# VectorE's table and angle steps dealt into other places of the gate loop, one pair of gathers exchanged, and the first loads cut smaller, in a four-layer AdaLN/FFN kernel

## The chip, the cores and the metric

The kernel runs on one core of one Trainium2 chip, in one launch. The metric is the device time of that core in microseconds (us). A core has TensorE (PE; its weight loads are listed apart as PEld), VectorE (DVE), ScalarE (ACT), GpSimd (POOL) and SyncE (SP). Transfers (DMAs) are issued from the queues of SP, ACT and POOL. Each engine works through its own instructions in order and waits on semaphores for the others.

## The reference

Eight sequences of 128 tokens of width 512 pass four layers, each of two steps, each layer added to its input:

```python
x = x + _L0_ffn_ref(_L0_cond_ref(x, ..., itok_B_2_6, 0), ...)
x = x + _L1_ffn_ref(_L1_cond_ref(x, ..., itok_B_3_7), ...)
x = x + _L2_ffn_ref(_L2_cond_ref(x, ..., itok_Bx16_0_63, itok_B_207_1644), ...)
x = x + _L3_ffn_ref(_L3_cond_ref(x, itok_B_0_7, ...), ...)
```

The change touches the inside of two of them. The first step of layer 0 is a gated feed-forward net of width 1376 with a low-rank adapter per sequence:

```python
def lora_add(base, inp, A, B):
    Ab = A[layer_idx][lora_indices]
    Bb = B[layer_idx][lora_indices]
    t = jnp.einsum('bri,bni->bnr', Ab, inp)
    return base + jnp.einsum('bor,bnr->bno', Bb, t) * SCALE
gate = lora_add(jnp.einsum('bnh,fh->bnf', x, W_gate), x, A_gate, B_gate)
up = lora_add(jnp.einsum('bnh,fh->bnf', x, W_up), x, A_up, B_up)
act = jax.nn.silu(gate) * up
down = lora_add(jnp.einsum('bnf,hf->bnh', act, W_down), act, A_down, B_down)
```

The first step of layer 2 is attention over a paged cache: queries and keys are normed and rotated by position, cached keys and values are found by a block table, and cached positions beyond a sequence's length are masked:

```python
pos = cache_seqlens[:, None] + jnp.arange(seqlen)[None, :]
q = _rope(q, pos)
k = _rope(k, pos)
kc = k_cache[block_table].reshape(bsz, L, HK, D)
vc = v_cache[block_table].reshape(bsz, L, HK, D)
```

The other layers are adapters and routed mixtures; the change reaches them only through two small tables (`mask1`, `bias3`).

## The kernel before

All of x stays on the chip, turned: four chunks `c` of 128 features by 1024 tokens. A quarter is 256 tokens.

*Start.* SP loads the first 512 tokens chunk by chunk (L85), the adapter numbers `ids0_i` behind the first chunk (L88), then the remaining 512 tokens in one load of 1 MB (L89) and the weights of gate block 1 (L80). ACT loads the weights of block 0 in two pieces each for gate and up: chunk 0, then chunks 1 to 3. Loads from SP and ACT draw on the same eight semaphores, in turn, so that a load's issue waits until the load eight places earlier has landed. TensorE runs five matmuls on zeros (`idle`) and then block 0 (`gates`): for quarters 0 and 1, then 2 and 3, chunk by chunk, gate and up weights against each quarter. From `ids0_i` VectorE works out a row per partition, and GpSimd gathers the adapters' rows (Ag, Au, Bg, Bu, Ad, Bd).

*Tables.* `ints` loads the other id lists and turns them to floats (L134). From them VectorE builds `mask1`, `bias3` and, for values and for keys, the row numbers of the cache (`selp`, `page`, eight `kvrow` slices each, L180 to L191). They stand in the program ahead of the gate loop.

*Gate loop.* Blocks f = 1 to 10 of 128 hidden features (`gates_by_seven`) use Strassen's seven products. A block has for each of two groups `g` the banks `one`, `two` and `six`. TensorE runs the first products of both groups; VectorE makes three sums for each group from them (L456, L457, L459: six sums); TensorE then adds further products into the same banks, for which it must wait until VectorE has read them; the low-rank parts follow; then VectorE makes ten operations (L474 to L479) with ACT's Silu. Those ten run while TensorE is in the next block. The eight banks of PSUM go round, six to a block. GpSimd forms the weight sums of the next block (`weight_sums`, L429), and once, after block 5, sums of the down weights (L520). The order within each engine is written out by hand (`kept`). The rotation angles (`rotary`: `pos`, `ang`, then the reduction for sine and cosine, then small scalings of the norm weights) are 23 VectorE steps, dealt three at a time to the end of the blocks from f = 2 on.

*Attention.* 32 steps, each one group of heads for two sequences. A step n is prepared one step ahead: its projection (`project`, seven products again, `q_one`, `q_six`, `q_five`) and the product with the output weights of the step before (`leave`, `wo_one`, `wo_two`, `wo_six`) stand between the scores of two sequences. Cached keys are gathered by GpSimd (`gather(n, "k")`, eight indirect DMAs into `kn`), transposed by VectorE (`turn_cached`, L1111) and turned by a trip through memory; cached values are gathered into `vals`. GpSimd also makes the crossed rotation terms (`vq`, `vk`, L1070). At the start, `run` issues `gather(1, "v")` ahead of step 0, and `gather(2, "k")` in the middle of step 0; step 2's keys are transposed inside step 2's projection, which stands in step 1 (the entry "c22" there).

Of the kernel before, what the change touches and what calls it, by code (L numbers as in the profile page):

```python
# [10 lines left out]
F32 = mybir.dt.float32  # L11
I32 = mybir.dt.int32
AF = mybir.ActivationFunctionType
ALU = mybir.AluOpType
AX = mybir.AxisListType
PSUM = bass.MemoryType.PSUM

P = 128
NB = 8
NT = NB * P  # L20
D = 512
DC = D // P
# [6 lines left out]
NQ = 8  # L29
# [18 lines left out]
def forward(ctx: ExitStack, tc: tile.TileContext, a: dict, out: bass.AP):  # L48
    nc = tc.nc
    pe, act, dve, pool, sp = nc.tensor, nc.scalar, nc.vector, nc.gpsimd, nc.sync  # L50
# [23 lines left out]
    def gate_weights(f, by=sp, parts=(slice(0, DC),)):  # L74
        fw = min(P, FF - f * P)
        fs = slice(f * P, f * P + fw)
        ws = [st.tile([P, DC, P], F32, tag="w" + n, name=f"w{n}_{f}") for n in "gu"]
        for cs in parts:
            for n, w in zip("gu", ws):
                by.dma_start(w[:, cs, :fw], a[f"W{n}T"].rearrange("(c p) o -> p c o", p=P)[:, cs, fs])  # L80
        return ws

    ids0_i = const.tile([P, NB], I32, tag="lora_ids_i", name="lora_ids_i")
    for c in range(DC):
        sp.dma_start(x[:, c, 0:512], a["xT"][c * P : (c + 1) * P, 0:512])  # L85
        if c == 0:
            first = gate_weights(0, act, (slice(0, 1), slice(1, DC)))
            sp.dma_start(ids0_i, a["lora_ids"].partition_broadcast(P))  # L88
    sp.dma_start(x[:, :, 512:NT], a["xT"].rearrange("(c p) t -> p c t", p=P)[:, :, 512:NT])  # L89
    second = gate_weights(1)  # L90
# [39 lines left out]
    def ints(name, n, where=const):  # L130
        ti = where.tile([P, n], I32, tag=name + "_i", name=name + "_i")
        sp.dma_start(ti, a[name].partition_broadcast(P))
        tf = where.tile([P, n], F32, tag=name, name=name)
        dve.tensor_copy(tf, ti)  # L134
        return tf

    def rows(name, n, where=const):
        t = where.tile([P, n], F32, tag=name, name=name)
# [31 lines left out]


    mask1 = const.tile([P, NB], F32, tag="mask1", name="mask1")
    dve.tensor_scalar(mask1, ids1, p_div16, None, ALU.is_equal)

    kvrow = {}
    for what, order in (("v", "p (b c j) -> p b c j"), ("k", "p (b j c) -> p b c j")):
        selp = w0.tile([P, NB, 4, 4], F32, tag="selp", name="selp_" + what)
        dve.tensor_tensor(  # L180
            selp,
            table.rearrange(order, b=NB, c=4),
            block32.unsqueeze(1).unsqueeze(1).to_broadcast([P, NB, 4, 4]),
            ALU.mult,
        )
        page = const.tile([P, NB * 4], F32, tag="page", name="page_" + what)
        dve.tensor_reduce(page.rearrange("p (b c) -> p b c", c=4), selp, AX.X, ALU.add)
        dve.tensor_scalar(page, page, 32.0, p_mod32, ALU.mult, ALU.add)
        kvrow[what] = const.tile([P, NQ, NB * 4], I32, tag="kvrow_" + what, name="kvrow_" + what)
        for qd in range(NQ):  # L190
            dve.tensor_scalar(kvrow[what][:, qd, :], page, float(NQ), float(qd), ALU.mult, ALU.add)  # L191


    bias3 = const.tile([P, NB, 8], F32, tag="bias3", name="bias3")
    dve.tensor_tensor(
        bias3,
        eight.unsqueeze(1).to_broadcast([P, NB, 8]),
        lang.unsqueeze(2).to_broadcast([P, NB, 8]),
        ALU.is_equal,
    )  # L200
    dve.tensor_scalar(bias3, bias3, 5.0, None, ALU.mult)


    def load_small(dst_pool, name, shape, src, tag=None, bufs=None):
# [113 lines left out]
    with c0:  # L318
# [36 lines left out]
        def quarter(j):  # L355
            return slice(j * NT // 4, (j + 1) * NT // 4)
# [4 lines left out]
        def mmq(o, lhsT, rhs, start, stop):  # L361
            pe.matmul(o, lhsT, rhs, start=start, stop=stop, skip_group_check=True)  # L362
# [31 lines left out]
        def gates(f, ws, between):  # L394

            fw = min(P, FF - f * P)
            banks = [bank(f"gu_{f}_{j}") for j in range(4)]
            for js in ((0, 1), (2, 3)):
                for c in range(DC):
                    if js[0] and c == 2:  # L400
                        between()
                    for k, w in enumerate(ws):
                        for j in js:
                            mmq(banks[j][:fw, k, :], w[:, c, :fw], x[:, c, quarter(j)], k == 0 and c == 0, False)
            return banks


# [21 lines left out]
                kept(by.tensor_tensor(o, l, r, op))  # L429
            return a11, a12, a22, s1, s2, s3, s4  # L430

        def gates_by_seven(f, A):

            fw = min(P, FF - f * P)
            fs = slice(f * P, f * P + fw)
            a11, a12, a22, s1, s2, s3, s4 = A

            def into(o, l, r, start):
                for c in range(2):
                    mmq(o, l[:, c, :], r[:, c, :], start and c == 0, False)  # L440

            def new(name, g):
                return st.tile([P, NT // 4], F32, tag=f"{name}{g}", name=f"{name}_{f}_{g}", bufs=1)[:fw]

            B = []
            for g in range(TG):
                b11, _, b21, b22 = token_blocks(g)
                t1, t2, t3, t4 = (xs[:, g, k] for k in range(4))
                one, two, six = (bank(f"{n}_{f}_{g}")[:fw] for n in ("g1", "g2", "g6"))
                into(one[:, 0], a11, b11, True)  # L450
                p1 = new("p1", g)
                kept(act.copy(p1, one[:, 0]))
                into(two[:, 0], s2, t2, True)
                into(two[:, 1], s1, t1, False)
                u = new("u", g)
                kept(dve.tensor_tensor(u, two[:, 0], p1, ALU.add))  # L456
                kept(dve.tensor_tensor(p1, two[:, 1], p1, ALU.add))  # L457
                into(six[:, 0], s3, t3, True)
                kept(dve.tensor_tensor(p1, six[:, 0], p1, ALU.add))  # L459
                B.append((one, two, six, p1, u, b21, b22, t4))  # L460
            for one, two, six, _, _, b21, b22, t4 in B:
                into(one[:, 0], a12, b21, False)
                into(two[:, 1], s4, b22, False)
                into(six[:, 0], a22, t4, False)

            for (W, t), at in (((Bg, tgm), ((0, 0), (1, 1))), ((Bu, tum), ((2, 0), (1, 0)))):
                for g in range(TG):
                    for i, (k, h_) in enumerate(at):
                        j = 2 * g + i
                        mmq(B[g][k][:, h_], W[slot(j), fs], t[slot(j), :], False, True)  # L470
            for g, (one, two, six, p1, u, _, _, _) in enumerate(B):
                g1, g2, up = new("g1", g), new("g2", g), new("up", g)
                kept(act.activation(g1, one[:, 0], AF.Silu))
                kept(dve.tensor_tensor(up, six[:, 0], u, ALU.add))  # L474
                kept(dve.tensor_tensor(g2, two[:, 1], u, ALU.add))
                kept(act.activation(g2, g2, AF.Silu))
                kept(dve.tensor_tensor(p1, two[:, 0], p1, ALU.add))
                kept(dve.tensor_tensor(h[:fw, f, quarter(2 * g)], g1, up, ALU.mult))
                kept(dve.tensor_tensor(h[:fw, f, quarter(2 * g + 1)], g2, p1, ALU.mult))  # L479
# [58 lines left out]
        banks = gates(0, first, lora_in)  # L538
        lora_gates(0, banks)
        rot, angles, turn_angles = rotary(tc, rp, w0, lens, part, rows, kept)  # L540
        for f in range(1, NF):
            after = f + 1 < NF and weight_sums(f + 1, gate_weights(f + 1))
            gates_by_seven(f, A)
            A = after
            if f == 2:
                down_loaded()
            for i in itertools.islice(angles, 3 * (f > 1)):
                kept(i)
            if f == NF // 2:
                AW = [down_weights(0, wop.tile([P, 3, NH, P], F32, tag="os", name="wds_0"))]  # L550
        cg.close()
# [241 lines left out]
def attention(tc, a, x, ident, lens, kvrow, part, ww, wop, ypool, sums, rot, eps, psa, c2, chunks, mm):  # L793
# [66 lines left out]
    def kept(i):  # L860
        return tc.keep_in_program_order(i) if running or i.ins.engine == pool.engine else i
# [42 lines left out]
    def gather(n, what):  # L904
        qd, p = steps[n]
        t = []
        for j in range(2):
            if what == "k":
                d = kvp.tile([P, 4, HD], F32, tag="kn", name=f"kn_{n}_{j}")
            else:  # L910
                d = vals[n % 2 * 2 + j]
            for c in range(4):
                i = (2 * p + j) * 4 + c
                kept(pool.indirect_dma_start(  # L914
                    out=d[:, c, :], out_offset=None, in_=kc if what == "k" else vc,
                    in_offset=bass.IndirectOffsetOnAxis(ap=kvrow[what][:, qd, i : i + 1], axis=0),
                ))
            t.append(d)
        S[n][what + "c"] = t
# [398 lines left out]
    def run(pool_, end_of, bank, keep):  # L1318
# [4 lines left out]
        squared(1)  # L1323
        keys_terms()
        roots(1)
        gather(1, "v")
        rotated(1)
        normed(1)
        end, prepared = None, iter(())
# [5 lines left out]
        for n, (qd, p) in enumerate(steps):  # L1335
# [40 lines left out]
            summed(n, 0)  # L1376
            if n == 0:
                next(sums_of)
                gather(2, "k")
            every(sums_of)  # L1380
            if n == 0:
                turn_at_once(1)
# [943 lines left out]
```

## Time and profile before

| What | Value |
| --- | --- |
| five runs | 1490.86, 1491.67, 1494.53, 1495.07, 1501.02 us |
| median | 1494.53 us |
| the profiled execution | 1491.0 us |
| its span | 1489.2 us |
| TensorE clock granted, mean | 0.999 |
| VectorE, ACT, GpSimd busy | 72%, 38%, 57% |

The span runs from the first to the last instruction of one execution. The table of busy times counts an engine as busy while an instruction of its runs. The waits list says for each instruction on an engine what ended the idle time before it, in sum, times and longest. In a timeline a row is: start, duration, engine, source line, operation, what it writes and reads, shape, count, and in brackets the idle time before it with what ended it.

The chain of work that ended last, by engine:

```profile
PE 92%; DVE 3%; POOL 2%; DMA 1%; issue 1%; ACT 0%; SPq 0%; DVEq 0%; POOLq 0%; ACTq 0%
```

### The profile page before, as it was taken

The page shows a single profiled execution, that of the slowest core. Times are in us where ns is not written, and L with a number is a line of the kernel's source. Part 1 is how long each engine was busy: PE and PEld are TensorE (multiplying, and loading weights), DVE is VectorE, ACT ScalarE, POOL GpSimd, SP SyncE. Part 2 cuts the span into 40 slices and gives each one's busy share as a digit, 9 for nine tenths or more (in the row PEclk, how much of TensorE's full clock was granted, in tenths as well). Part 3 has the DMA queues.
Part 4 walks back from the last instruction along what each step waited for, and adds up shares of the span by engine and source line. Part 5 has one row for each costly group of instructions (what it writes and reads, how often), then busy time and mean ns, then how long its engine had stood idle before and what let it go on. Part 6 is the DMA issues. An engine that isn't in the chain of part 4 may idle for free.

```text
span 1489.2 us, 18090 instructions
## 1 busy us (share of the span) xinstructions
PE 1475.5 (99%) x5603; PEld 937.9 (63%) x5603; DVE 1067.7 (72%) x2121; ACT 561.9 (38%) x1422; POOL 854.4 (57%) x876
## 2 busy tenths in 40 slices
PE   9999999999999999999999999999999999999998
PEld 7888787455555655555565555555555556559886
DVE  5665524388888787877778778777877878855475
ACT  1111101044444554454454444455445445431110
POOL 2242103567776777777677777677777767632310
PEclk9999999999999999999999999999999999999999
DMA  7411001213546434554444445444445534333001
GB/s 242 118 44 32 1 1 55 94 35 113 169 140 197 138 122 131 156 178 134 135 150 120 129 151 181 126 135 152 131 129 160 170 116 135 111 116 98 1 9 52
DMA packets 155081, 171.44 MB, mean 115 GB/s; under 512 B 52576, under 2 KB 125472, under 8 KB 154848
## 3 DMA queue, kind: packets, MB, share of 16 engines
q1 hardware_dynamic: 136832, 133.18, 30.0%
q0 software_dynamic: 17056, 36.49, 7.6%
q8 instruction: 47, 0.77, 0.2%
q10 hardware_dynamic: 1088, 0.52, 0.1%
q14 instruction: 58, 0.48, 0.1%
HBM read 129.36 MB, written 40.76 MB: 114 GB/s over the span
## 4 chain that ended last, share of the span: by engine, by line
PE 92%; DVE 3%; POOL 2%; DMA 1%; issue 1%; ACT 0%; SPq 0%; DVEq 0%; POOLq 0%; ACTq 0%
PE st L1165 17%; PE av L1217 17%; PE g L362 8%; PE q_six L971 8%; PE wo_two L971 5%; PE q_one L971 5%; PE q_five L971 5%; PE dn L362 5%; PE wo_six L971 4%; PE wo_one L971 4%; PE eo_l L53 3%; PE h L1753 2%; PE z L1753 2%; PE o L1753 1%; PE midp_l L53 1%; PE gu L362 1%
## 5 line engine op out<-in xcount | busy, mean ns | idle before, releaser
L914 POOL DMA_INDIRECT kn<-in_k_cache,kvrow_k x256 | 270.0, 1055 | 77.6 <-issue 67.8
L914 POOL DMA_INDIRECT vals<-in_v_cache,kvrow_v x256 | 271.4, 1060 | 73.5 <-issue 49.9
L1217 PE MATMUL av<-pT,vals 128*128 128x512 f32 x640 | 290.7, 592 | 0.2 <-DVE oT L1227 0.2
L1169 ACT ACTIVATE pT<-st,hide 128x512 f32<-128x512 f32 x256 | 175.9, 687 | 191.0 <-PE st L1165 190.9
L1165 PE MATMUL st<-qT,kT 128*128 128x512 f32 x512 | 235.9, 593 | 0.7 <-DMA qT<-turned_new 0.6
L1217 PEld LDWEIGHTS av<-pT,vals 128*128 128x128 f32 x640 | 121.4, 190 | 152.7 <-issue 147.1
L1070 POOL TENSOR_TENSOR vq<-q,txq 128x256 f32<-128x256 f32 x128 | 121.2, 976 | 134.9 <-ACT sqq L1044 96.2
L1165 PEld LDWEIGHTS st<-qT,kT 128*128 128x128 f32 x512 | 96.7, 190 | 109.5 <-issue 102.7
L1185 DVE TENSOR_TENSOR part<-pT 128x512 f32<-128x512 f32 x128 | 88.3, 691 | 77.1 <-ACT pT L1169 73.2
L971 PE MATMUL q_one<-q,x 128*128 128x384 f32 x256 | 93.0, 486 | 0.0
L1044 ACT ACTIVATE sqq<-q 128x128 f32<-128x128 f32 x252 | 78.1, 310 | 13.2 <-DVE q L1020 6.5
L971 PEld LDWEIGHTS q_one<-q,x 128*128 128x128 f32 x256 | 48.5, 190 | 39.8 <-issue 14.1
L971 PE MATMUL q_six<-q_s,xs_all 128*128 128x384 f32 x192 | 69.8, 486 | 0.0
L1025 ACT COPY q<-q_one 128x256 f32<-128x256 f32 x32 | 11.9, 372 | 148.9 <-PE q_one L971 142.8
L971 PE MATMUL wo_one<-o,oT 128*128 128x256 f32 x256 | 65.8, 379 | 0.6 <-DVE oT L1227 0.6
L1165 PE MATMUL st<-qT,kTn 128*128 128x512 f32 x128 | 65.4, 592 | 0.0
L971 PE MATMUL wo_two<-o_s,os 128*128 128x256 f32 x256 | 60.6, 380 | 1.7 <-DVE vals L1020 1.5
L1169 ACT ACTIVATE pT<-st,rs 128x512 f32<-128x512 f32 x64 | 44.0, 687 | 38.5 <-PE st L1165 38.5
L971 PEld LDWEIGHTS wo_one<-o,oT 128*128 128x128 f32 x256 | 48.6, 190 | 14.2 <-DVE oT L1227 0.8
L429 POOL TENSOR_TENSOR ws<-wu 128x256 f32<-128x256 f32 (+1 forms) x9 | 6.4, 712 | 87.8 <-DMA wu<-in_WuT 81.4
L1201 ACT COPY rows<-rows 32x32 f32<-32x32 f32 x96 | 20.7, 216 | 92.7 <-DVE rows L1196 91.9
L362 PE MATMUL g<-xs,ws 128*128 128x256 f32 (+1 forms) x240 | 55.1, 379 | 0.0
(461 smaller groups left out, 2841.3 us busy)
## 6 DMA issues: line engine op xcount, KB each, us to landing
turned_new<-qkt SPq DMA_DIRECT2D x120, 160.0 KB
turned_cached<-kt SPq DMA_DIRECT2D x128, 128.0 KB
kT<-turned_cached SPq DMA_DIRECT2D x32, 512.0 KB
R<-sums SPq DMA_DIRECT2D x32, 512.0 KB
qT<-turned_new SPq DMA_DIRECT2D x30, 512.0 KB
q<-in_WqT SPq DMA_DIRECT2D x8, 1024.0 KB
o<-in_WoT SPq DMA_DIRECT2D x8, 1024.0 KB
kn<-in_k_cache,kvrow_k POOLq DMA_INDIRECT x256, 2.8
```

Source lines behind the costliest of these rows:

```text
L53: pe.matmul(o, lhsT, rhs, start=start, stop=stop)
L362: pe.matmul(o, lhsT, rhs, start=start, stop=stop, skip_group_check=True)
L914: kept(pool.indirect_dma_start(out=d[:, c, :], out_offset=None, in_=kc if what == "k" else vc, in_offset=bass.IndirectOffsetOnAxis(ap=kvro ...
L971: kept(pe.matmul(o, l[:, c, :], r[:, c, :], start=start and c == 0, stop=c == 1, skip_group_check=True))
L1044: kept(act.activation(sq, S[n][m][:, j, i, :], AF.Square, accum_out=S[n]["ssq"][:, j, col : col + 1]))
L1070: kept(pool.tensor_tensor(to, t[:, b, :, hi : hi + 64], wx[:, b, lo : lo + 64].unsqueeze(2).to_broadcast(list(to.shape)), ALU.mult,))
L1165: kept(pe.matmul(ps, s["kT"][:, c, 4 * j : 4 * j + 4, :] if c < 4 else s["kn"][:, j], s["qT"][:, :, REP * j : REP * (j + 1), :].rearrange( ...
L1169: kept(act.activation(pT[:, c, :, :].rearrange("p i t -> p (i t)"), ps, AF.Exp, **(dict(bias=hide[:, b, c : c + 1]) if c < 4 else dict(bia ...
L1185: kept(dve.tensor_tensor(o, l, r, ALU.add))
L1201: kept(act.copy(rows[0:32, g, :], rows[32 * g : 32 * g + 32, 0, :]))
L1217: kept(pe.matmul(ps, v[:, c, :], pT[:, c, :, :].rearrange("p i t -> p (i t)"), start=c == 0, stop=c == NC - 1, skip_group_check=True,))
L1753: return pe.matmul(o, lhsT, rhs, start=start, stop=stop, skip_group_check=True)
```

## The change

- The first chunk of the first 512 tokens is loaded in two halves, and for that chunk and those two quarters TensorE takes gate and up of quarter 0, then of quarter 1. Block 0's weights come in three pieces each (chunk 0, chunk 1, chunks 2 and 3). The adapter numbers are loaded behind token chunk 1.
- The tables become a generator `tables()` of 29 VectorE operations, the conversions of the ids among them. `gates_by_seven` takes an iterator `meanwhile` and issues its operations behind the block's six sums. Blocks 1 and 2 get 15 and 14 table operations there, blocks 3 to 10 three angle steps each.
- `run` gathers step 2's keys where it gathered step 1's values, and step 1's values where it gathered step 2's keys.

```diff
     for c in range(DC):
-        sp.dma_start(x[:, c, 0:512], a["xT"][c * P : (c + 1) * P, 0:512])
+        for t in (slice(0, 256), slice(256, 512)) if c == 0 else (slice(0, 512),):
+            sp.dma_start(x[:, c, t], a["xT"][c * P : (c + 1) * P, t])
         if c == 0:
-            first = gate_weights(0, act, (slice(0, 1), slice(1, DC)))
+            first = gate_weights(0, act, (slice(0, 1), slice(1, 2), slice(2, DC)))
+        if c == 1:
             sp.dma_start(ids0_i, a["lora_ids"].partition_broadcast(P))
...
-        dve.tensor_copy(tf, ti)
+        to_float.append((tf, ti))
...
+    def tables():
+
+        for tf, ti in to_float:
+            yield dve.tensor_copy(tf, ti)
+        yield dve.tensor_scalar(mask1, ids1, p_div16, None, ALU.is_equal)
+        yield dve.tensor_tensor(
+            bias3,
...
+        yield dve.tensor_scalar(bias3, bias3, 5.0, None, ALU.mult)
+        for what, order in (("v", "p (b c j) -> p b c j"), ("k", "p (b j c) -> p b c j")):
+            selp = w0.tile([P, NB, 4, 4], F32, tag="selp", name="selp_" + what)
+            yield dve.tensor_tensor(
+                selp,
...
+            yield dve.tensor_reduce(page.rearrange("p (b c) -> p b c", c=4), selp, AX.X, ALU.add)
+            yield dve.tensor_scalar(page, page, 32.0, p_mod32, ALU.mult, ALU.add)
+            for qd in range(NQ):
+                yield dve.tensor_scalar(kvrow[what][:, qd, :], page, float(NQ), float(qd), ALU.mult, ALU.add)
...
-                    for k, w in enumerate(ws):
-                        for j in js:
-                            mmq(banks[j][:fw, k, :], w[:, c, :fw], x[:, c, quarter(j)], k == 0 and c == 0, False)
+                    order = [(k, j) for k in range(2) for j in js]
+                    if c + js[0] == 0:
+                        order.sort(key=lambda at: at[1])
+                    for k, j in order:
+                        mmq(banks[j][:fw, k, :], ws[k][:, c, :fw], x[:, c, quarter(j)], k == 0 and c == 0, False)
...
-        def gates_by_seven(f, A):
+        def gates_by_seven(f, A, meanwhile):
...
                 B.append((one, two, six, p1, u, b21, b22, t4))
+            for i in meanwhile:
+                kept(i)
             for one, two, six, _, _, b21, b22, t4 in B:
...
+        tabled = tables()
         for f in range(1, NF):
             after = f + 1 < NF and weight_sums(f + 1, gate_weights(f + 1))
-            gates_by_seven(f, A)
+            gates_by_seven(f, A, itertools.islice(tabled, 15) if f < 3 else itertools.islice(angles, 3))
             A = after
             if f == 2:
                 down_loaded()
-            for i in itertools.islice(angles, 3 * (f > 1)):
-                kept(i)
...
-        gather(1, "v")
+        gather(2, "k")
         rotated(1)
...
                 next(sums_of)
-                gather(2, "k")
+                gather(1, "v")
```

## The prediction

> **What bounds the kernel now.** I read the busy times first, then TensorE's waits, then the timelines around each wait.
>
> ```profile
> PE 1475.5 (99%) x5603; PEld 937.9 (63%) x5603; DVE 1067.7 (72%) x2121; ACT 561.9 (38%) x1422; POOL 854.4 (57%) x876
> ...
> PE wo_two L971 <- DVE vals L1020: 1.5, 1, 1.5
> PE idle L53 <- DVE ramp L104: 1.2, 1, 1.2
> PE g L362 <- DVE p L457: 0.9, 1, 0.9
> PE zT L2159 <- DVE zg L2146: 0.8, 2, 0.5
> PE st L1165 <- DMA qT<-turned_new: 0.6, 1, 0.6
> ```
>
> TensorE sets the time: of the 1489.2 us span it is without work for 13.7. No matmul is added or removed here, so all that can be won is idle TensorE time at the places touched. Two of the listed waits lie there (wo_two, and g in the gate loop), and a third (qT) follows the first. The windows of the gate blocks give the loop's stalls more exactly than the list:
>
> ```profile
> 26.11:39.47 13.36, 13.36 (x76) 11.28 (x73) 3.96 (x10) 2.19 (x7) 2.81 (x4) 1.00 0.35 102
> ...
> 79.55:94.03 14.48, 13.60 (x76) 11.20 (x72) 10.19 (x19) 2.12 (x7) 10.20 (x8) 1.00 0.14 38
> ...
> 107.39:121.12 13.73, 13.60 (x76) 11.20 (x72) 9.44 (x19) 2.12 (x7) 3.51 (x4) 1.00 0.22 58
> ```
>
> Columns: window, its sum, then busy time (instructions) of PE, PEld, DVE, ACT, POOL. A full block takes 13.36 us. Block f=5 takes 14.48 and f=7 takes 13.73, so 1.12 + 0.37 = 1.49 us is lost, in these two alone. Why, VectorE's timeline of block 5 shows:
>
> ```profile
> 83.51 1.21 DVE L1455 SCALAR_TENSOR_TENSOR r_sin<-k_sin,r_sin 128x512 f32<-128x512 f32 x1
> 84.75 1.10 DVE L1456 SCALAR_TENSOR_TENSOR r_sin<-k_sin,r_sin 128x512 f32<-128x512 f32 x1
> 85.89 1.64 DVE L1459 TENSOR_SCALAR r_sin<-r_sin 128x512 f32<-128x512 f32 x1
> 87.45 0.41 DVE L456 TENSOR_TENSOR u<-g,p 128x256 f32<-128x256 f32 x1
> 87.90 0.42 DVE L457 TENSOR_TENSOR p<-g,p 128x256 f32<-128x256 f32 x1
> ...
> 94.12 0.43 DVE L474 TENSOR_TENSOR up<-g,u 128x256 f32<-128x256 f32 x1 [3.95 <-PE g L362]
> ```
>
> Three angle steps stand ahead of the block's six sums (L456 to L459) and take 3.94 us while GpSimd works beside them. TensorE would be at the matmuls behind the first sums at 87.42, and starts them at 88.47. After the six sums VectorE is then idle 3.95 us until the next block's ten operations.
>
> The second place is step 2's projection:
>
> ```profile
> 340.09 1.12 POOL L914 DMA_INDIRECT kn<-in_k_cache,kvrow_k x1 [0.30 <-issue]
> ...
> 349.50 0.95 POOL L914 DMA_INDIRECT kn<-in_k_cache,kvrow_k x1 [0.30 <-issue]
> ...
> 352.13 0.71 DVE L1111 STREAM_TRANSPOSE kt<-kn 128x512 f32<-128x512 f32 x1 [1.49 <-DMA kn<-in_k_cache,kvrow_k]
> 353.68 0.28 DVE L1020 TENSOR_TENSOR vals<-q_five,uq 128x128 f32<-128x128 f32 x1
> ...
> 354.10 1.97 PE L971 MATMUL wo_two<-o_s,os 128*128 128x256 f32 x8 [1.47 <-DVE vals L1020]
> ```
>
> Step 2's keys are gathered behind step 1's values, their last piece lands at 352.0, VectorE's second transposition waits 1.49 us for it, and what is queued behind it includes the sum that frees wo_two's bank.
>
> **Angles and tables (two moves, one answer).** The angle groups move from ahead of a block's six sums to behind them. In an undisturbed block (f=9) the six sums end 7.8 us after the block's start (142.31 - 134.48), and the next ten operations start at 13.36 + 0.09: 5.6 us free, which is the idle time that the trace shows ahead of L474 wherever no angles are steered in (5.60 to 5.62, four times). The dearest group took 3.94 us, beside GpSimd's sums; a group of 128x512 steps alone takes 3 x 0.43 = 1.3 us by the rows at 99.68 and 100.14. Both fit. In block 5 GpSimd works on until 91.9 (the down weights' sums), so I price the group there at 3.94: from 87.4 to 91.3, before 93.0 (79.55 + 13.45). Were the 5.6 us overrun, the next block would still bear some 2.3 us: the first bank that waits for VectorE's ten operations is the second group's `two`-bank, reused by a matmul 3.45 us into the block and freed by the third operation 1.1 us after their start. So the 1.49 us go, and nothing comes back.
>
> The 29 table operations leave the stretch 15.0 to 21.9 us, where VectorE waited for id loads and held nobody up (tgm starts 1.41 us idle, on TensorE). Behind the six sums of block 1 stand 15 of them: casts 0.17+0.16+0.17+0.23, mask 0.23, bias 0.22+0.19, selp 0.28, reduce 0.28, page 0.24, five kvrow at 0.77/8 = 0.10 each: 2.7 us. In block 2: 3 x 0.10 + 0.37 + 0.29 + 0.24 + 0.78 = 2.0 us. Both in 5.6 us; the id loads have landed by 18.0. The first reader of a row table (the first gather of keys) comes after the gate loop, whose last block ends at 161.15. Cost 0. Without that cover the price is 2.7 + 2.0 = 4.7 us.
>
> **Gathers swapped.** GpSimd issues the same 16 gathers from 328.3 to 350.45; now the eight of keys come first, their last issued at about 338.8 and landed by 341.5 (2.7 us median), 8 us before VectorE's first transposition at 349.95. Its 1.49 us wait goes: transpositions 349.95 and 350.59, o_s 351.23, q 351.80, vals 352.14 to 352.42. wo_one ends at 352.46, and wo_two can start at 352.63, 1.47 us earlier. Step 1's values land by 350.45 + 2.5 = 353; TensorE reads them at 361.93 - 1.47 = 360.5, so 7 us of slack. What is late next: the turned queries. GpSimd's vq waits for VectorE's q (353.90) and starts the chain vq, vk, rotated, transposition, write, read (qT lands at 372.95, TensorE waited 0.60). GpSimd is free at 350.45, q is there at 352.3, so this chain moves by the same 1.5 us as TensorE: the 0.60 stays. Bounds: it goes too (-0.6), or the chain does not move at all (+1.47). I take 0, as every link up to vq's start is in the rows.
>
> **First tokens and weights.** The first block's tokens are halved, the first matmuls go by halves, and the weights' chunk 1 gets its own loads: one more issue on SP, two more on ACT, some 0.4 to 0.5 us each.
>
> ```profile
> 4.75 0.34 PEld L53 LDWEIGHTS idle<-nought 128*128 128x128 f32 x1
> 5.18 0.34 PEld L362 LDWEIGHTS gu<-x,wg 128*128 128x128 f32 x1
> ...
> 11.59 0.69 DVE L418 TENSOR_TENSOR xs<-x 128x512 f32<-128x512 f32 x1 [0.82 <-DMA x<-in_xT]
> ```
>
> The first gate weights load at 5.18, 0.43 us behind the last of the five warming matmuls, the spacing at which these run too: TensorE didn't wait for tokens, and the warming matmuls stay. Gain 0. The possible loss: eight DMA semaphores go round in order, so a ninth load waits for the first's landing. Before, the 1 MB of remaining tokens (L89) was issued at 4.36, behind the first tokens; now it waits for the weights' chunk 1. It landed at 11.56; TensorE reaches the third quarter of the tokens at 13.16 (weight loads every 0.86 us from 7.98 on), 1.6 us later. The nearest row for that chunk is wu's first 64 KB, issued 1.17 and landed by 5.46 (SP's wait ends there): 4.3 us, so 1.66 + 4.3 = 6.0, and with the same 7.2 us from issue to landing 13.2: just in time. If the chunk lands only when the whole 192 KB did (7.5), it is 14.7: 1.5 us late. The weights' last two chunks are likewise held until wg's and wu's first landed (4.0 and 5.46); with the 5.9 us that 192 KB took (1.66 to 7.5) wu's would be there at 11.3, needed at 10.57: 0.8 late. Bounds 0 and 1.5 us. I take 0: these loads carry 128 KB, not 192, and from 5 to 11 us the DMA engines moved some 370 GB/s without a gap, so landings went by the bytes queued ahead, which stay the same. By the Trainium skill (DMA: Bandwidth & Descriptors, Anatomy of one DMA) a load has about 2 us fixed plus its bytes at 436 GB/s, an estimate of 2.2 us for 64 KB; that would have the chunk land at 3.9, with a cost of 0 and no chance for rival 1. The trace's 4.3 us disagrees, so rival 1 keeps its chance.
>
> The lora ids move from 1.18 to behind token chunk 1 (landed by 6.37), so the six gathers of adapter rows come up to 1.2 us later. Au landed 6.3 us after 8.53 and is needed at 17.15; Bu 11.5 after 11.28, needed at 25.36: 2.3 and 2.6 us of slack. Cost 0.
>
> **Sum.** -1.49 - 1.47 + 0 = -2.96 us. The profiled execution took 1491.0 (span 1489.2) and would take 1488.0. It is among the faster ones; the median of the five is 1494.53, so I forecast 1491.6.
>
> **Rivals.**
> 1. *The start gives some back.* The remaining tokens or the weights' last chunks come late: 0.8 to 1.5 us, 1.2 in the middle, so 1492.8. For: the 4.3 us row. Against: the engines' full load. Chance 0.15.
> 2. *The waited-for keys give way to the waited-for queries.* The chain to qT doesn't move: -1.49 only, 1493.0. For: the chain has six links and its margin is negative already (0.60). Against: its first link starts at VectorE's q. Chance 0.15.
> 3. *Slower: VectorE becomes a block's bound from behind.* A group behind the six sums runs over its 5.6 us and holds the ten operations that free the banks. It decides from 5.6 + 2.3 = 7.9 us on, and to eat 2.96 us over eight blocks it must be 8.3 us. At 9 us: 8 x 1.1 - 2.96 = +5.8, 1500.4. For: a step of 0.43 us took 1.64 beside GpSimd. Against: the dearest group is 3.94, and GpSimd stops some 6 us into each block but one. Chance 0.05.
> 4. *Both waits and qT's go:* 1491.0. Chance 0.1.
>
> The forecast itself has 0.55. Single runs of the kernel spread over 10 us, so a median of five can be off by 2 to 4 whatever the change does; with rivals 1, 2 and 4 that gives 1487.5 to 1496.5. About 0.5% (7.5 us) is what a measurement of this kernel can tell from no change: the forecast (-0.2%) and rivals 1, 2 and 4 lie within it; beyond it on the fast side lies only a lucky median (0.07), on the slow side rival 3 and an unlucky one (0.06).
>
> **What would show it.** All ten gate blocks at 13.3 to 13.4 us, VectorE's idle stretch ahead of L474 shrunk by the groups, no TensorE wait on p L457; no wait of L1111 on step 2's kn and none of wo_two on vals; qT's wait near 0.6; first gate weights again at about 5.2 us and no wait in front of the third and fourth token quarters. A block above 13.4, a new wait before 26 us, or a wait on qT of 2 us would prove a step wrong; a median outside 1487.5 to 1496.5 the sum.

## The result, and the profile after

| | before | after |
| --- | --- | --- |
| median | 1493.82 us (71 runs, 1489.05 to 1501.02) | 1490.72 us (41 runs, 1487.19 to 1494.71) |
| profiled execution, its span | 1491.0, 1489.2 us | 1489.5, 1487.7 us |

The ratio is 0.9979 with an interval of 0.9973 to 0.9984: 3.1 us less (2.4 to 4.0, the interval times 1493.8). The two profiled spans differ by 1.5 us only. TensorE's waits in the changed kernel (what waited, on what; sum, times, longest, in us):

```profile
PE st L1173 <- DMA qT<-turned_new: 1.5, 2, 1.1
PE idle L53 <- DVE ramp L106: 1.2, 1, 1.2
PE zT L2167 <- DVE zg L2154: 0.8, 2, 0.5
PE gu L367 <- DMA x<-in_xT: 0.7, 1, 0.7
```

The two waits that the change aimed at, wo_two on vals and g on p, are gone. The one on qT has grown from 0.6 to 1.5 in sum, and a new one stands in the first block: gu on the remaining tokens. The windows of gate blocks 1, 5 and 7 of the changed kernel:

```profile
26.70:40.06 13.36, 13.36 (x76) 11.28 (x72) 7.52 (x25) 2.19 (x7) 2.88 (x4) 1.00 0.45 147
80.14:93.50 13.36, 13.36 (x76) 11.28 (x72) 11.10 (x19) 1.84 (x6) 10.08 (x8) 1.00 0.15 41
106.86:120.22 13.36, 13.36 (x76) 11.28 (x72) 8.39 (x19) 2.12 (x7) 3.10 (x4) 1.00 0.21 59
```

All ten blocks take 13.36 us (the short last one 13.31), so the loop is 1.49 us shorter. But its first block begins at 26.70, where it began at 26.11. Block 5 again, in VectorE's timeline of the changed kernel:

```profile
87.55 0.42 DVE L466 TENSOR_TENSOR p<-g,p 128x256 f32<-128x256 f32 x1
87.96 1.16 DVE L1463 SCALAR_TENSOR_TENSOR r_sin<-k_sin,r_sin 128x512 f32<-128x512 f32 x1
89.15 1.91 DVE L1464 SCALAR_TENSOR_TENSOR r_sin<-k_sin,r_sin 128x512 f32<-128x512 f32 x1
91.09 1.65 DVE L1467 TENSOR_SCALAR r_sin<-r_sin 128x512 f32<-128x512 f32 x1
93.59 0.42 DVE L483 TENSOR_TENSOR up<-g,u 128x256 f32<-128x256 f32 x1 [0.85 <-PE g L367]
```

The angles now stand behind the last of the six sums. Beside GpSimd they take 4.78 us, and 0.85 us are left until TensorE releases the next ten operations.

Step 2's projection and the turned queries, in the timelines of VectorE and TensorE:

```profile
349.19 1.29 DVE L1119 STREAM_TRANSPOSE kt<-kn 128x512 f32<-128x512 f32 x2
...
351.31 0.28 DVE L1028 TENSOR_TENSOR vals<-q_five,uq 128x128 f32<-128x128 f32 x1
...
351.73 0.45 PE L979 MATMUL wo_two<-o_s,os 128*128 128x256 f32 x1
...
371.11 1.10 PE L1173 MATMUL st<-qT,kT 128*128 128x512 f32 x2 [1.08 <-DMA qT<-turned_new]
```

No bracket stands behind the transpositions or wo_two: both waits have gone. The wait on qT was 0.60 here and is 1.08. In all, +0.59 at the start, -1.49 in the loop, -1.47 at wo_two, +0.48 at qT in step 2 and +0.37 at a later wait on qT make -1.5, which is what the two spans show.

The start, in the timelines of TensorE and VectorE of the changed kernel:

```profile
13.86 1.13 PE L367 MATMUL gu<-x,wg 128*128 128x256 f32 x4 [0.74 <-DMA x<-in_xT]
...
23.08 0.42 DVE L436 TENSOR_TENSOR ws<-wu 128x256 f32<-128x256 f32 x1 [6.62 <-DMA wu<-in_WuT]
...
24.55 0.41 DVE L374 TENSOR_TENSOR tgm<-t,half 128x256 f32<-128x256 f32 x1
```

The remaining tokens land at 13.84, where they landed at 11.56. Block 1's weights land at 23, where they landed at 15. Behind them VectorE makes the four weight sums and then tgm, which is done 0.7 us before TensorE needs it at 25.63. So the landings are late by up to 8 us, in a kernel that loads the same bytes.

**How one profile stands to the median.** TensorE's order behind step 2's gathers is the same in all kernels of this study, save for what comes late. So the table compares the profiled executions at four places: where block 1 begins, where the gate loop ends (first matmul of wb1T), wo_two, and the first matmul of alp, behind everything that was changed. Times are differences from the execution of before.

| Run | block 1 (26.11) | loop's end (161.15) | wo_two (354.10) | alp (503.12) | span (1489.2) |
| --- | --- | --- | --- | --- | --- |
| the whole change | +0.59 | -0.90 | -2.37 | -1.75 | -1.5 |
| start alone (e1) | +2.16 | +3.67 | +3.79 | +3.44 | +6.8 |
| loop alone (e2) | -0.48 | -1.97 | -1.74 | -1.48 | +2.1 |
| gathers alone (e3) | +1.60 | +3.28 | +2.08 | +1.41 | +9.4 |
| without the start (e4) | +0.12 | -1.38 | -1.83 | -2.60 | +1.6 |
| tables alone (e5) | +0.79 | +1.14 | +1.28 | +0.89 | +3.9 |
| angles alone (e6) | -0.66 | -2.15 | -2.02 | -2.66 | -1.9 |
| without the halves (e7) | -0.12 | -1.62 | -3.21 | -3.91 | -1.1 |
| without the pieces (e8) | +1.57 | +0.08 | -1.51 | -1.30 | -0.5 |
| before, late gathers (e9) | +0.53 | +0.62 | +0.66 | +0.05 | +3.9 |
| after, late gathers (e10) | -0.37 | -1.86 | -2.26 | -3.24 | +1.8 |
| e4, late gathers (e11) | -0.66 | -2.15 | -3.34 | -3.46 | -1.5 |

Behind alp, where nothing was changed, every one of the twelve lost time against the execution of before: 0.3 us (the whole change) to 8 us (e3, +9.4 less +1.41). The profiled execution of before took 2.8 us less than its kernel's median, that of the changed kernel 1.2 us less than its own; that is why the spans show less than the medians, and one execution can't say where a median one loses the difference. e3's profiled execution is the slowest of that kernel's twelve runs. Verdicts below go by the medians, mechanisms by the first four columns.

### The profile page after: what moved, and what is told of

Its sections match the earlier page's. It is cut to its first block, busy times and chain, and to the rows that moved or that the text cites. A ratio compares the mean times of both kernels' runs of the same rounds, so it can differ in the third digit from the quotient of the medians.

```text
span 1487.7 us, 18093 instructions
## 1 busy us (share of the span) xinstructions
PE 1475.5 (99%) x5603; PEld 937.2 (63%) x5603; DVE 1065.1 (72%) x2121; ACT 562.2 (38%) x1422; POOL 854.7 (57%) x876
## 4 chain that ended last, share of the span: by engine, by line
PE 93%; DVE 3%; DMA 2%; issue 0%; ACT 0%; SPq 0%; ACTq 0%; DVEq 0%
PE st L1173 18%; PE av L1225 17%; PE g L367 9%; PE q_six L979 8%; PE q_one L979 6%; PE q_five L979 6%; PE wo_two L979 5%; PE dn L367 5%; PE wo_one L979 4%; PE wo_six L979 3%; PE eo_l L53 3%; PE h L1761 2%; PE z L1761 2%; PE o L1761 1%; PE midp_l L53 1%; DMA qT<-turned_new 1%
## 5 line engine op out<-in xcount | busy, mean ns | idle before, releaser
L979 PEld LDWEIGHTS q_one<-q,x 128*128 128x128 f32 x256 | 48.5, 190 | 39.8 <-issue 14.4
```

The costliest lines, as they stand in the source:

```text
L979: kept(pe.matmul(o, l[:, c, :], r[:, c, :], start=start and c == 0, stop=c == 1, skip_group_check=True))
```

## Experiments

Each ratio is to the kernel before, run beside it on the same chip. It is an estimate of its own, with an interval of 95%, and can differ from the quotient of the two medians by up to 0.001. Every kernel here computes the whole reference. The change has three parts: the start (halved tokens, weight pieces, adapter numbers loaded later), the loop (tables and angles behind the six sums) and the gathers (keys ahead of values).

**e1: the start alone.**

```diff
-        sp.dma_start(x[:, c, 0:512], a["xT"][c * P : (c + 1) * P, 0:512])
+        for t in (slice(0, 256), slice(256, 512)) if c == 0 else (slice(0, 512),):
+            sp.dma_start(x[:, c, t], a["xT"][c * P : (c + 1) * P, t])
...
-            first = gate_weights(0, act, (slice(0, 1), slice(1, DC)))
+            first = gate_weights(0, act, (slice(0, 1), slice(1, 2), slice(2, DC)))
+        if c == 1:
             sp.dma_start(ids0_i, a["lora_ids"].partition_broadcast(P))
...
+                    if c + js[0] == 0:
+                        order.sort(key=lambda at: at[1])
```

> Only the loads at the start and the order of the first matmuls are changed; tables, angles and gathers stand as before. Forecast's theory: nothing gained, nothing lost, ratio 1.0000 within 0.0004, and TensorE comes to gate block 1 at about 26.1 us. Rival 1 (the remaining tokens come late): TensorE waits 0.5 to 1.5 us ahead of the third token quarter and the ratio is 1.0003 to 1.0010. A third theory, that the halved load does speed the start: block 1 begins before 25.7 us, ratio below 0.9997.

Measured: 1500.04 us against 1496.68, ratio 1.0020 (1.0002 to 1.0037). The start alone is slower, though the interval only just leaves out no change. Its waits:

```profile
PE gu L364 <- DVE tgm L371: 1.9, 1, 1.9
PE wo_two L975 <- DVE vals L1024: 1.5, 1, 1.5
PE st L1169 <- DMA qT<-turned_new: 1.3, 2, 1.1
PE idle L53 <- DVE ramp L106: 1.2, 1, 1.2
PE g L364 <- DVE p L461: 1.0, 1, 1.0
```

The first one is new. VectorE's and TensorE's timelines of e1 tell what tgm waited for:

```profile
21.32 0.17 DVE L136 CAST adapter_ids<-adapter_ids_i 128x8 f32<-128x8 int32 x1 [6.33 <-DMA adapter_ids_i<-in_adapter_ids]
21.40 0.42 DVE L433 TENSOR_TENSOR ws<-wu 128x256 f32<-128x256 f32 x1
...
25.79 0.78 DVE L193 TENSOR_SCALAR kvrow_k<-page_k 128x32 int32<-128x32 f32 x8
26.48 0.42 DVE L371 TENSOR_TENSOR tgm<-t,half 128x256 f32<-128x256 f32 x1
...
26.95 0.71 PE L364 MATMUL gu<-tgm,Bg 32*128 32x256 f32 x8 [1.89 <-DVE tgm L371]
```

The ids landed at 21.3 where they had landed at 15.0. From then to 26.48 VectorE converts them, sums the weights and makes the tables without a pause, and only then tgm. So the tables stand in the way as soon as the small loads are late. And the price nearly doubles, as e1's windows show (third column from the right: granted clock):

```profile
27.00:28.00 1.00, 1.00 (x16) 0.67 (x16) 0.23 (x1) 0.00 (x0) 0.00 (x0) 0.87 0.63 193
28.00:29.00 1.00, 1.00 (x6) 0.65 (x3) 0.25 (x1) 0.67 (x3) 0.00 (x0) 0.50 1.07 320
29.00:30.00 1.00, 1.00 (x4) 0.82 (x3) 1.00 (x4) 0.54 (x2) 0.00 (x0) 0.50 0.71 203
30.00:31.00 1.00, 1.00 (x4) 0.73 (x4) 0.16 (x1) 0.37 (x1) 0.00 (x0) 0.50 0.10 26
31.00:32.00 1.00, 1.00 (x6) 0.90 (x5) 0.00 (x0) 0.00 (x0) 0.00 (x0) 0.93 0.05 12
```

Behind the stop TensorE runs at half its clock: 0.26 + 3 + 0.14 = 3.4 us of it (twice what each slice lacks to 1.00), which is 1.7 us of work lost. Block 1 takes 14.76 instead of 13.36.

**e2: the loop alone** (the table and angle parts of the diff above, nothing else).

> Only tables and angle steps move behind the six sums. Forecast's theory: blocks 5 and 7 go from 14.48 and 13.73 us to 13.36, so 1.5 us less, ratio 0.9990; no TensorE wait on VectorE's p in the gate loop. Rival (VectorE bound from behind): blocks above 13.4 us, ratio 1.000 or more.

Measured: 1495.52 us, ratio 0.9990 (0.9978 to 1.0002). All ten blocks at 13.36, -1.49 between the first two columns of the table; wo_two's wait is still there (1.60). The loop's mechanism holds. Its gain in the median can't be told from nothing, by a hair.

**e3: the gathers alone.**

```diff
-        gather(1, "v")
+        gather(2, "k")
...
-                gather(2, "k")
+                gather(1, "v")
```

> Only the two gathers are exchanged. Forecast's theory: wo_two's wait of 1.47 us on vals goes and qT's stays near 0.6, so 1.5 us less, ratio 0.9990. Rival 2 (the queries take the keys' place): qT's wait grows to about 2 us, ratio 1.000. Between the two, qT's wait near 1.1 as in the changed kernel's profile: 1.0 us less, ratio 0.9993.

Measured: 1496.21 us, ratio 0.9996 (0.9982 to 1.0009). wo_two's wait on vals fell from 1.47 to 0.27, and in step 2 no matmul waits for qT, so the turned queries came earlier with it. This kernel is the kernel before up to 328 us, and yet in its profiled execution the ids came late too (VectorE's and TensorE's timelines of e3):

```profile
20.46 0.17 DVE L134 CAST adapter_ids<-adapter_ids_i 128x8 f32<-128x8 int32 x1 [5.67 <-DMA adapter_ids_i<-in_adapter_ids]
...
26.16 0.42 DVE L369 TENSOR_TENSOR tgm<-t,half 128x256 f32<-128x256 f32 x1
...
26.63 0.71 PE L362 MATMUL gu<-tgm,Bg 32*128 32x256 f32 x8 [1.74 <-DVE tgm L369]
```

So the landing at 15.0 in the profile of before was one outcome among several of the same program. A stop of 1.74 us follows, and then 3.4 us at half clock: block 1 takes 15.05.

**e4: the loop and the gathers, with the start of before.**

> Loop and gathers as in the changed kernel, the start as before. Forecast's theory: the same as the changed kernel, ratio 0.998 to before. Rival 1: the changed kernel's start costs 0.6 us or more, so this one is faster than it, ratio 0.9975. If the halved start gains, this one is slower than the changed kernel, ratio 0.9984 or above.

Measured: 1493.38 us, ratio 0.9974 (0.9961 to 0.9986), beside 0.9979 (0.9973 to 0.9984) for the whole change. Where the tables have moved, the start is worth nothing that shows, though alone it cost some 3 us (1496.7 times 0.002; 0.3 to 5.5 by the interval). That fits a harm that goes through the tables, as e1's trace shows it at work; it isn't proven, since e3, with the start of before, shows the same stop.

In e4 the swap's gain at wo_two is mostly gone again. TensorE's timeline:

```profile
351.33 1.10 PE L975 MATMUL wo_one<-o,oT 128*128 128x256 f32 x4 [0.79 <-ACT k L1029]
```

Instead of the wait on vals, one of 0.79 us on ACT's copy of k stands just ahead of wo_two: between loop's end and wo_two the table shows -0.45 instead of -1.47. e10 (0.94 us, -0.40) and e12 (0.94 us) have it too, the other five kernels with the swap and the six without it don't. Why ACT's copy was late in these three is open.

**e5: the tables alone** (the angles stay ahead of the sums).

> Only the tables move behind the six sums of blocks 1 and 2; angles, gathers and start as before. Forecast's theory: the tables held nobody up, ratio 1.0000 within 0.0004. New theory, from the profiles of the start alone and of the gathers alone (id loads landed at 20 to 21 us instead of 15, VectorE reached tgm at 26.2 to 26.5 and TensorE waited 1.7 to 1.9 us for it): in a part of the executions the tables stand in front of tgm, and moving them wins up to 1.9 us there, on the median 0.5 to 1.5 us, ratio 0.9990 to 0.9997; this profile shows no TensorE wait on tgm.

Measured: 1493.18 us, ratio 0.9994 (0.9983 to 1.0005). tgm has no tables ahead of it and VectorE is idle 8.25 us before it. But another load was late in the profiled execution, one of the adapter rows that GpSimd gathers. e5's waits:

```profile
PE wo_two L977 <- DVE vals L1026: 1.5, 1, 1.5
PE g L365 <- DVE p L460: 1.4, 2, 0.9
PE AuT L349 <- DMA Au<-in_Au,row_i: 1.3, 1, 1.3
```

What moving the tables wins by itself in the median stays open: between 0.17% won and 0.05% lost. No kernel here has the angles and the gathers without the tables.

**e6: the angles alone** (the tables stay where they were).

```diff
-            gates_by_seven(f, A)
+            gates_by_seven(f, A, () if f < 3 else itertools.islice(angles, 3))
...
-            for i in itertools.islice(angles, 3 * (f > 1)):
-                kept(i)
```

> Only the angle steps move. Forecast's theory: all of the loop's 1.5 us, ratio 0.9990, blocks 5 and 7 at 13.36 us. New theory: the same in the blocks, and TensorE may still wait for tgm when the id loads land late, ratio 0.9990 to 0.9994 all the same, since only the tables cure that.

Measured: 1492.31 us, ratio 0.9991 (0.9981 to 1.0002). All ten blocks at 13.36. Here the ids landed at 14.86, tgm was there at 22.59, and TensorE didn't wait for it. The 1.49 us of the loop are the angles' alone.

**e7 and e8: the changed kernel without the halved tokens, and without the third weight piece.**

```diff
-        for t in (slice(0, 256), slice(256, 512)) if c == 0 else (slice(0, 512),):
-            sp.dma_start(x[:, c, t], a["xT"][c * P : (c + 1) * P, t])
+        sp.dma_start(x[:, c, 0:512], a["xT"][c * P : (c + 1) * P, 0:512])
```

> The changed kernel without the halved tokens: chunk 0 in one load, gate and up in the old order; the weights' three pieces, the later adapter numbers, loop and gathers stay. If the halves (one more load in the round of eight) are what makes the remaining tokens late: landing before 12.5 us, ratio 0.9972 to 0.9977, faster than the changed kernel (0.9979). If the three pieces are: about 0.9979 with a wait for the third quarter of about 1 us. If neither costs anything, no difference to either.

```diff
-            first = gate_weights(0, act, (slice(0, 1), slice(1, 2), slice(2, DC)))
+            first = gate_weights(0, act, (slice(0, 1), slice(1, DC)))
```

> The changed kernel with block 0's weights in two pieces as before; halves, later adapter numbers, loop and gathers stay. TensorE should wait again for the 192 KB piece where its clock rises early (1.1 to 1.6 us in two profiles), and the remaining tokens are issued behind the first 64 KB, near 4.4 us, and land before 12.5. If the pieces win more than they cost: ratio 0.9980 to 0.9986, slower than the changed kernel. If they cost more: 0.9972 to 0.9977.

Measured: 1489.98 us, ratio 0.9977 (0.9966 to 0.9988), and 1491.41 us, ratio 0.9983 (0.9972 to 0.9993). Neither differs measurably from the whole change. The profiles show different loads late: in e7 block 1's weights (22.1 us), in e8 the gathered Au, for which TensorE stood 2.2 us, while those weights were there at 14.9. Either what SP loads or what GpSimd gathers comes late, and no edit of the start decided which in a way that the medians show.

The traces, though, sort by one edit. VectorE's first sum of block 1's weights begins at 19.5 to 23.1 us in all five kernels with three weight pieces (the whole change, e1, e7, e10, e12). With two pieces it begins at 14.2 to 15.3 in seven (before, e2, e4, e5, e6, e8, e11) and at 19.7 and 20.5 in two (e9, e3). With one execution of each kernel this is a hint that the third piece makes the late landing more frequent, which would be the link from the start to the tables in e1; it isn't shown.

**e9 to e11: two of GpSimd's gathers later.** Ad and Bd (967 KB) are first read at 164 us. They are issued behind the sums of block 3's weights instead of at the start: in the kernel before (e9), in the changed one (e10), and in that of e4 (e11).

```diff
-        Ad, Bd = gathered("Ad", FF), gathered("Bd", D)
...
             if f == 2:
                 down_loaded()
+                Ad, Bd = gathered("Ad", FF, kept), gathered("Bd", D, kept)
```

> The kernel before, with the two gathers of the down adapters (Ad and Bd, 967 KB, issued at some 12.5 us, first read at 164 us) issued by GpSimd behind the sums of block 3's weights instead of at the start. Theory A (the small loads of ids and tables, and the second block's weights, land at 15 us in some executions and at 20 to 23 in others because they share the DMA engines with what GpSimd gathers; where they are late, the tables hold tgm and TensorE 1.7 to 1.9 us, and block 1 another 1.4 to 1.7): at some 370 GB/s 967 KB are 2.6 us, so the small loads land by about 18 at the latest, tgm is in time, block 1 is 13.36, no wait of PE on tgm; ratio 0.997 to 0.999. Blocks 5 and 7 keep 14.48 and 13.7. Theory B (lateness has nothing to do with these bytes): ids still land at 15 or at 20, ratio 0.9995 to 1.0005.

> The changed kernel with the same two gathers issued behind the sums of block 3's weights. Theory A: block 1's weight wu, which landed at 22 to 23 us in the changed kernel, lands by 20, the wait for the remaining tokens (1.15 us, issued 5.60, landed 13.84) stays, since they land before Ad is issued; gate block 1 begins at 25.6 to 26.2 instead of 26.70, blocks 13.36; ratio 0.9965 to 0.9980. Theory B: block 1 begins at 26 to 27, ratio 0.998 as the changed kernel has.

> The loop and the gather parts of the change with the start of the kernel before, and the two gathers of the down adapters issued behind the sums of block 3's weights. If the start part is worth nothing once the tables have moved, this is as fast as the changed kernel or faster: ratio 0.9960 to 0.9980. If the start part is worth 0.5 us or more, it is at or above the changed kernel with late gathers in the same call by 0.0003 or more.

Measured: 1492.53, 1490.72 and 1490.62 us against 1492.79, ratios 0.9994 (0.9983 to 1.0006), 0.9976 (0.9963 to 0.9989) and 0.9985 (0.9974 to 0.9996). From e9's timeline of VectorE:

```profile
19.59 0.17 DVE L134 CAST adapter_ids<-adapter_ids_i 128x8 f32<-128x8 int32 x1 [3.38 <-DMA adapter_ids_i<-in_adapter_ids]
...
24.72 0.42 DVE L368 TENSOR_TENSOR tgm<-t,half 128x256 f32<-128x256 f32 x1
```

In e9 TensorE doesn't wait for tgm, and in e10 block 1 begins at 25.74, as theory A said. But the ids still land at 19.6, later than the 18 that it asked for, and the time of e9 is that of the kernel before, as theory B said. So these bytes are not what makes the small loads late, or not alone, and a queue kept shorter wins nothing measurable. e11 settles nothing about the start: its ratio is 0.0009 above e10's, its median 0.1 us below, and the intervals overlap. No version of this study beats the changed kernel beyond the intervals.

**e12: eighteen more VectorE steps behind the six sums of blocks 3 to 10.**

```diff
             for i in meanwhile:
                 kept(i)
+            for _ in range(18 * (f > 2)):
+                kept(dve.tensor_tensor(nought, nought, nought, ALU.add))
```

> The changed kernel with 18 more VectorE additions of a 128x256 tile of zeros behind the six sums and the three angle steps of each of blocks 3 to 10 (0.335 us from start to start by the rows of the changed kernel: 6.0 us; with the angles' 1.3 us 7.3 us). By the prediction's threshold (5.6 us free and 2.3 us that the next block bears, 7.9 together) the blocks stay 13.36 and the time that of the changed kernel (ratio 0.998). If the 5.6 us alone were the threshold, each of the eight blocks grows by 1.7 us: 14 us, ratio 1.007. If VectorE's own work bounds a run of such blocks (ten operations 3.7, six sums 2.9, angles 1.3, zeros 6.0, in all 13.9 against 13.36), each grows by about 0.5 us: 4 us, ratio 1.001; and by more where GpSimd slows VectorE.

Measured: 1527.90 us, ratio 1.0230 (1.0212 to 1.0248): 34 us slower, more than any of the three theories gave. One cause is mine: the load was 11.3 us a block (9.96 + 1.3), not 7.3, since the additions cost more than 0.335 us each. The first block that feels it still tests the threshold. e12's timelines of VectorE, GpSimd and TensorE there:

```profile
62.20 6.39 DVE L471 TENSOR_TENSOR nought<-nought 128x256 f32<-128x256 f32 x14
68.63 3.53 DVE L471 TENSOR_TENSOR nought<-nought 128x256 f32<-128x256 f32 x4
...
68.57 0.72 POOL L436 TENSOR_TENSOR ws<-wu 128x256 f32<-128x256 f32 x1 [10.13 <-DMA wu<-in_WuT]
...
72.09 0.41 DVE L485 TENSOR_TENSOR up<-g,u 128x256 f32<-128x256 f32 x1
...
66.49 1.13 PE L367 MATMUL g<-x,wg 128*128 128x256 f32 x4
...
72.55 1.36 PE L367 MATMUL g<-x,wg 128*128 128x256 f32 x4 [2.34 <-DVE up L485]
```

The first fourteen additions, each on the tile that the one before wrote, take 0.46 us each; the last four, from the start of GpSimd's weight sums on, take 0.88 us each. The ten operations were due 0.09 us behind the block's start (66.49), and began at 72.09: 5.51 us late. TensorE stood 2.34 us. So 3.2 us were borne, not 2.3: the bank is freed by the first of the ten (L485, done at 72.50), not by the third. Again the clock follows, in e12's windows:

```profile
70.00:72.55 2.55, 0.21 (x1) 0.00 (x0) 2.48 (x5) 0.00 (x0) 1.88 (x3) 1.00 0.00 0
73.00:77.00 4.00, 4.00 (x13) 3.20 (x12) 3.68 (x11) 1.66 (x5) 0.00 (x0) 0.57 0.00 0
78.00:82.00 4.00, 4.00 (x20) 3.52 (x19) 3.69 (x10) 0.00 (x0) 0.00 (x0) 1.00 0.01 2
```

Within 73 to 77 the granted clock is 0.57, which takes 1.7 us of the 4 (0.43 x 4). The block lasts 17.65 instead of 13.36: 2.34 us of stop, and nearly as much again of slower clock. In the six blocks behind it VectorE has hardly a pause left (17.6 to 19.1 us busy of each 20 from 80 to 180 us), and they take 14.4 to 20.5 us. The seven take 17.4 on average, near the 17.9 that VectorE's work now adds up to (3.7 + 2.9 + 1.3 + some 10): this is the third theory's bound, with the additions at their measured price. The loop grew by 28 us in all; another 8.2 us TensorE stood behind it, for ACT's copy of wb1T, for which the last block's ten operations came late.

## Why the prediction held, and which step failed

- **The sum** was -2.96 us, and the medians say -3.1 (-4.0 to -2.4). It is right, but made of terms of which one was wrongly reasoned. That it agrees so closely is in part luck: the interval also holds rival 4 (-3.6), though not rivals 1 (-1.8) and 2 (-1.5), and no part by itself has an interval that leaves out no change on the fast side (e1, e2, e3, e5, e6). The traces show the two gains; the medians show only that the loop and the gathers together win (e4).
- **Angles: right.** -1.49 us, to the hundredth, in the changed kernel, e2 and e6; no wait on p is left in them. The group in block 5 took 4.78 us where I had priced 3.94, with 0.85 us to spare.
- **Tables: the step that failed.** I priced them at nothing, because VectorE "waited for id loads and held nobody up". That was read from one execution in which the ids landed at 15.0. In e1 and e3, which keep the tables ahead of tgm, they landed at 21.3 and 20.5, and the tables held TensorE 1.9 and 1.7 us, with the half clock 3.5 and 3.4 us in all. The changed kernel lost nothing there, though its weights landed at 23: tgm was in time by 0.7 us, with the four weight sums still ahead of it. How much of the median that wins isn't shown (e5 alone: nothing that can be told).
- **Gathers: the wait went** as worked out: the wait on vals is 0.27 us or gone in all eight executions with the swap, with the keys' transpositions unhindered. What TensorE wins by wo_two varies: 1.5 to 1.6 us in the changed kernel, e7 and e8, 1.2 in e3 and e11, 0.4 in e4 and e10, where the wait on ACT's k takes its place. That "the 0.60 stays" at qT is not what happened, but neither is rival 2. With the swap, step 2 waits 1.08, 0.72 and 0.62 us for qT (the changed kernel, e8, e11), and no matmul waits there in e3, e4, e7, e10 and e12; without it 0.60, 0.22 and 0.81 (before, e1, e2), and none in e5, e6 and e9. A chain that stood still would show a wait of some 2 us in each. So the chain moves with TensorE, and the wait comes and goes with either order.
- **Start: mis-sized in the profile, right in the median.** I took 0 because landings "went by the bytes queued ahead". The remaining tokens were issued 1.24 us later and landed 2.3 us later (13.84; my bound was 13.2 to 14.7). TensorE got to them at 12.7 instead of 13.16, for its early weight loads ran faster in this execution (as in e2's, with the start of before). The wait was rival 1 in place and kind. It cost 0.59 us at block 1's start; in the medians e4 shows no cost. The formula that the prediction puts beside the 4.3 us row (Trainium skill, DMA: Bandwidth & Descriptors, Anatomy of one DMA) is given there for loads that GpSimd issues; this one is issued by ACT, so the row doesn't contradict it. Alone, the start does cost (e1), by its trace through the tables, a link that I hadn't seen, since I priced each part against the kernel before and not against one another.
- **Rival 3** (VectorE bounds a block from behind) did not occur. Its threshold of 5.6 + 2.3 was too low by 0.9 us. Its price was too low as well: it left out that a stop of 2.3 us can cost nearly as much again by the clock (e12).

## What to carry to other kernels

Before a step off the critical path is priced at nothing, ask how late its inputs can land, and not only how late they landed in the one execution at hand: work that waits for small loads shouldn't stand ahead of work that TensorE waits for. A part of a change that costs alone may cost nothing once another part has taken away what it runs into, so the parts are priced together. Where a change touches a third of a kernel, compare profiles up to the last place touched, and leave the rest to medians.

## What the runs showed of the hardware

- Loads of one program land at very different times. The ids landed at 15.0 and 14.9 us (before, e6) and at 20.5 (e3), issued at 7.5, 7.4 and 7.9 us with the same instructions ahead of them, while the DMA engines moved 190 to 410 GB/s in every stretch of 2 us from 6 to 24 us.
- Stops of TensorE of 1.89, 1.74 and 2.34 us were followed, 0.7 to 1.3 us behind their end, by 3.4 us at a granted clock of 0.50 (e1, e3, e12). But a stop of 2.25 us in e8, for Au, and another of 2.25 us in e12 (up to 128.59) were not: the clock stayed at 1.00. So the length of the stop alone doesn't decide. By the Trainium skill (TensorE: Matmul & The Clock Gate, "Part 1: The HAM clock gate"), the clock is halved after an idle window of about 3.4 us and restored after a busy one of that length, and the windows run freely. The 3.4 us at half clock agree with these runs; the 3.4 us of idleness do not, since 1.74 us were enough.
- VectorE additions of 128x256 in a row on one tile started 0.46 us apart in e12, where operations of this size on different tiles start 0.33 us apart (its L485 to L490). Beside GpSimd's weight sums the same additions took 0.88 us each.
